# A graph layer and a mixture of experts on one core: one more expert's weights resident, search tables in the weight slots, pools that wait by tile, and a second pair kept for the tail

## The chip, the core and the metric

The kernel runs on one core of a Trainium2 chip. Its engines are TensorE (PE; PEld are its weight loads), VectorE (DVE), ScalarE (ACT), GpSimd (POOL) and SyncE (SP), each with a queue of its own that is worked through in order; SP, ACT and POOL also issue DMAs. The metric is the device time of one execution in microseconds (us), lower is better. The kernel before has a median of 478.54 us in three runs (478.29 to 480.56).

## The reference, cut to what matters

```python
# x (1024, 512); 16384 edges src -> dst with a weight; dst is sorted
HW  = layernorm(x) @ W
agg = segment_sum(edge_weight[:, None] * HW[src], dst) + bias
x   = x + relu(agg)

xt     = layernorm(x)                                # 1024 tokens
scores = sigmoid(xt @ Wg.T + bg)                     # 64 experts
w, idx = top_k(scores, 2);  w = w / w.sum(-1)
nx     = normalize(xt)
h1 = nx @ (gamma_e * W1_e) + (b1_e + beta_e @ W1_e)  # (512, 256) for each expert e
h3 = nx @ (gamma_e * W3_e) + (b3_e + beta_e @ W3_e)
y  = sum over the two chosen e of  w_e * ((silu(h1) * h3) @ W2_e + b2_e)
z  = a small shared expert of width 32 with (gs, bs, Ws1, bs1, Ws3, bs3, Ws2, bs2)
return x + y + z
```

Everything is float32. The experts' weights are 64 x 3 x 0.524 MB, just over 100 MB, each read once.

## The kernel before

**The graph part.** Tokens lie in 8 tiles of 128. The edges are searched in windows with tables (thr_row, diff, below, erows, sm, then d_w, s_w, e_w, blk_i, hi_i, part) that the pool "graph" (gp) holds. DVE writes one-hots of the edges (one_hots, L403 to L408), PE makes dense blocks of the adjacency matrix from them (matrix_group, L495), turns them (L505) and multiplies with H @ W (weighted_sum, L512). Tile by tile follow finish (L527, L528; the layer norm), scores (L556), choose (DVE: the two best experts), rank (how many earlier tokens took the same expert), put (a token's slot with its expert) and slots (one-hots of these). PE sums them (listed, L620) in plist, and from it DVE makes lists (L695) and tokens (L696): for every pair of experts 128 places, 64 for each expert, with the number of the token, or an invalid one where a place stays empty. nx_d in DRAM gets the normalized tokens.

**The expert part** runs over 33 positions n = 0 to 32, in an order written out by hand: 32 pairs of experts, and in position 24 one expert with the first block of tokens that have no place in a pair. Position n is called pair n below, whatever it holds. Each takes these steps:

- load_expert (L707, L708, L710, on SP's queue): W1 and W3 into one slot of tag w13, W2 into one of tag w2. The pool "weights" has AHEAD = 11 slots of each tag. The graph part uses the same slots for its big tables (big is w13, mid is w2), so that the first weights come as these tables are done with; after that a new expert waits until the expert 11 places earlier has been used: its w13 by xph, its w2 by xpy.
- fetch / gather (L721, POOL): 128 rows of nx_d by tokens, into one of four row tiles that are set to zero first (L717), four positions ahead.
- front / scaled: four transposes (L194, PE), then times gamma and plus beta (L733, L735, DVE), two positions ahead.
- hidden: a product for the biases (L746: bias_hm with two terms of the biases in bf16 over 128 partitions, bias_lo with the third over 64; for each of the two experts, so four matmuls), 16 records of xph (L750), silu (L753, ACT), mul (L755, DVE). Matmuls of the two experts of a pair run side by side in the two halves of the array.
- turned: two transposes (L762) and a copy (L764, ACT).
- back(n - 1): outputs of the position before (L772 on PE, 8 records; the copy xy, L775, ACT) and scatter (L779, POOL) of these rows to y_d in DRAM, which has two rows for each token and was set to zero near the start.

In the order of the program, position n has hidden(n), back(n - 1), extra work, turned(n), front(n + 2). Extra work is beyond (n = 2) and beyond_list (n = 4 to 11), which make the lists of tokens without a place, and "other outputs" (other_rows on DVE and ACT, other_turn L904, other_sum L911 and L912): the shared expert and the b2 of one tile, added to res. Two of these eight stand with weights() (the normalized top-2 weights, stored to w_d at L799) before front(0), the other six in three steps each from n = 13.

**The tail.** The last pair is not scattered: block_weights (POOL gathers the weights of its tokens) and block_hots (DVE, eight one-hots of 128 x 128) are made at n = 31. After the loop, y_d is read back in eight pieces (ys, L1010, alternating on ACT's and SP's queue), and waits for the scatter of n = 31. For each tile PE multiplies the one-hots with y (L1014), in odd tiles also a diagonal with ys (L1016); DVE adds the weighted ys rows (L1018, 12 times) and PE's sum (L1020, 8 times), and the tile is stored (L1021). A loop over further blocks without a place does not turn here.

Pools opened after the graph part (bp, gb, lp, psx) lie over the memory of the graph part's pools; their first use waits for those.

Of the kernel before, what the change touches and what calls it, by code (L numbers as in the profile page):

```python
# [9 lines left out]
F32 = mybir.dt.float32  # L10
I32 = mybir.dt.int32
# [7 lines left out]
P = 128  # L19
EPS = 1e-5  # L20
AHEAD = 11
# [3 lines left out]
def kernel(  # L25
# [111 lines left out]

    bias_hm = const.tile([P, 2 * H], BF16, name="bias_hm")
    bias_lo = const.tile([E, 2 * H], BF16, name="bias_lo")
    both = const.tile([P, E], BF16, name="both")  # L140
# [58 lines left out]
    with tc.tile_pool(name="graph", bufs=1) as gp, \  # L199
# [6 lines left out]
        def row_tile(name):  # L206
            return gp2.tile([P, D], F32, name=name, tag="row", bufs=6)

        with tc.manual_schedule(engines={ENG.PE, ENG.DVE, ENG.Activation, ENG.Pool}):

            nc.gpsimd.iota(iota, pattern=[[1, P]], base=0, channel_multiplier=0, allow_small_or_imprecise_dtypes=True)
            thr_row = gp.tile([P, NH, P], F32, name="thr_row")
# [5 lines left out]
            diff = gp.tile([P, P], F32, name="diff")  # L218
# [33 lines left out]
            below = gp.tile([P, NH, P], BF16, name="below")  # L252
# [8 lines left out]
            rows = gp.tile([P, NH, EJ], I32, name="erows")  # L261
# [45 lines left out]
            sm = gp.tile([P, NH, EJ], F32, name="sm")  # L307
# [7 lines left out]
            d_w = gp.tile([P, NH, P], I32, name="d_w")  # L315
            s_w = gp.tile([P, NH, P], I32, name="s_w")
            e_w = gp.tile([P, NH, P], F32, name="e_w")
# [18 lines left out]
            b13 = mid([P, 2, H], "b13", F32)  # L336
            for n in range(2):
                nc.gpsimd.dma_start(b13[n * E:(n + 1) * E, 0, :], b1)
                nc.gpsimd.dma_start(b13[n * E:(n + 1) * E, 1, :], b3)
# [29 lines left out]
            blk_i = gp.tile([P, NH, P], I32, name="blk_i")  # L369
            nc.vector.tensor_scalar(blk_i, d_w, 2, None, op0=ALU.logical_shift_right)  # L370
            nc.vector.tensor_scalar(d_w, d_w, DL - 1, None, op0=ALU.bitwise_and)
            hi_i = gp.tile([P, NH, P], I32, name="hi_i")
            nc.vector.tensor_scalar(hi_i, s_w, 5, None, op0=ALU.logical_shift_right)
            nc.vector.tensor_scalar(s_w, s_w, LO - 1, None, op0=ALU.bitwise_and)
            part = gp.tile([P, 3, NH, P], F32, name="part")
# [50 lines left out]
            row_b = gp.tile([P, P], I32, name="row_b")  # L426
# [56 lines left out]
        with tc.manual_schedule(engines={ENG.PE, ENG.DVE, ENG.Activation, ENG.Pool}):  # L483
# [255 lines left out]
    def hidden(xT, parts):  # L739
# [12 lines left out]
        a1 = bp.tile([P, H], F32, name="xa1")  # L752
        nc.scalar.activation(a1, ph[:, 0, :], AF.Silu)  # L753
        h = bp.tile([P, H], F32, name="xh")
# [3 lines left out]
    def turned(h):  # L758
        pt = psx.tile([P, HC, P], F32, name="xpht")
        v = h.rearrange("t (p c) -> t c p", c=HC)  # L760
        for c in range(HC):
            nc.tensor.transpose(pt[:, c, :], v[:, c, :], ident)  # L762
        hT = bp.tile([P, HC, P], F32, name="xhT")
        nc.scalar.copy(hT, pt)  # L764
        return hT

    def outputs(hT, parts):
# [6 lines left out]
        y = bp.tile([P, D], F32, name="xy")  # L774
# [15 lines left out]
    pick_o = const.tile([P, 1], BF16, name="pick_o")  # L790
# [17 lines left out]
    def beyond():  # L808
# [29 lines left out]
        nc.vector.tensor_mul(one, one, both)  # L838
        picked_o = lp.tile([P, 1], F32, name="picked_o")
        nc.vector.tensor_reduce(picked_o, one, AX.X, ALU.add)  # L840
        nc.vector.tensor_copy(pick_o, picked_o)
# [21 lines left out]
    def beyond_hots(c):  # L863

        hots = []
        for n in range(2):
            so = bp.tile([P, P], F32, name="oso", bufs=4)
# [18 lines left out]
    def other_rows(i):  # L886
        st = bp.tile([P, ZW], F32, name="st")
# [27 lines left out]
    def block_weights(numbers):  # L915
        w = bp.tile([P, 1], F32, name="bw", bufs=1)
# [6 lines left out]
    def block_hots(of, w):  # L923
        row = bp.tile([P, NT], F32, name="brel", bufs=1)
# [150 lines left out]
```

## Time and profile before

| | |
|---|---|
| median of three runs | 478.54 us |
| profiled execution, its own time | 480.64 us |
| its span, first to last instruction | 478.8 us |
| TensorE clock granted, mean | 0.965 |
| PE busy | 437.4 us, 91% of the span |
| DVE busy | 237.9 us, 50% |
| ACT, POOL busy | 97.8 us, 115.5 us |
| DMA | 132.52 MB, mean 277 GB/s |
| pair pace, n = 0 to 32 | 32 periods in 239.5 us |

Times in lines are microseconds from the start of the span. The profile cuts the span into 40 equal slices with a digit for the busy tenths of each engine; further views list what an engine waited for, groups of instructions by line, the chain of work that ended last, and the instructions of a stretch in order of time. In a line of the timeline stand start, duration, engine, line of the code, operation, what is written and read, and in brackets the idle time before it with what ended it. SPq, ACTq and POOLq are the queues' own entries, DMA issues among them.

### The profile page before, as it was taken

The page shows a single profiled execution, that of the slowest core. Times are in us where ns is not written, and L with a number is a line of the kernel's source. Part 1 is how long each engine was busy: PE and PEld are TensorE (multiplying, and loading weights), DVE is VectorE, ACT ScalarE, POOL GpSimd, SP SyncE. Part 2 cuts the span into 40 slices and gives each one's busy share as a digit, 9 for nine tenths or more (in the row PEclk, how much of TensorE's full clock was granted, in tenths as well). Part 3 has the DMA queues.
Part 4 walks back from the last instruction along what each step waited for, and adds up shares of the span by engine and source line. Part 5 has one row for each costly group of instructions (what it writes and reads, how often), then busy time and mean ns, then how long its engine had stood idle before and what let it go on. Part 6 is the DMA issues. An engine that isn't in the chain of part 4 may idle for free. (4 is left out here: it accounts for less than half of the span.)

```text
span 478.8 us, 6941 instructions
## 1 busy us (share of the span) xinstructions
PE 437.4 (91%) x2438; PEld 216.2 (45%) x2438; DVE 237.9 (50%) x725; ACT 97.8 (20%) x224; POOL 115.5 (24%) x148
## 2 busy tenths in 40 slices
PE   2999999999799996588999999999999999999782
PEld 1554995555455554333343443333433334534230
DVE  5979797402787777534743432323332332322265
ACT  1342223223421211101121121121121111211200
POOL 5533100000042223513123323323313323110200
PEclk9999999999999997599899999999999999999977
DMA  8296930232168539338999999999999999999194
GB/s 248 92 123 115 370 138 1 78 100 102 54 233 315 177 113 397 127 115 313 386 396 408 406 406 407 404 409 407 408 404 408 408 405 407 405 410 403 46 365 160
DMA packets 42296, 132.52 MB, mean 277 GB/s; under 512 B 8023, under 2 KB 8151, under 8 KB 42128
## 3 DMA queue, kind: packets, MB, share of 16 engines
q1 hardware_dynamic: 30464, 107.56, 58.4%
q0 software_dynamic: 8304, 18.17, 12.7%
q10 hardware_dynamic: 3488, 6.30, 3.6%
q8 instruction: 20, 0.33, 0.3%
q14 instruction: 20, 0.16, 0.1%
HBM read 124.00 MB, written 18.88 MB: 298 GB/s over the span
## 5 line engine op out<-in xcount | busy, mean ns | idle before, releaser
L750 PE MATMUL xph<-w,xT 128*64 128x512 f32 (+1 forms) x520 | 128.1, 606 | 1.8 <-DMA w<-in_L_ffn_W_dram 1.4
L779 POOL DMA_INDIRECT y_d<-xy,lists x31 | 32.8, 1057 | 168.3 <-ACT xhT L764 68.9
L750 PEld LDWEIGHTS xph<-w,xT 128*64 128x64 f32 (+1 forms) x520 | 39.0, 139 | 69.0 <-issue 66.1
L772 PE MATMUL xpy<-w,xhT 128*64 128x512 f32 (+1 forms) x260 | 67.4, 593 | 0.6 <-ACT xhT L764 0.6
L755 DVE TENSOR_TENSOR xh<-xa,xph 128x256 f32<-128x256 f32 x33 | 13.9, 420 | 106.3 <-ACT xa L753 106.3
L512 PE MATMUL acc<-hw,AT 128*128 128x512 f32 x128 | 60.6, 600 | 0.0
L495 PE MATMUL ph<-ov,ol 128*32 128x128 bf16 x768 | 48.1, 421 | 0.1
L753 ACT ACTIVATE xa<-xph 128x256 f32<-128x256 f32 x33 | 12.6, 383 | 152.9 <-PE xph L750 152.9
L495 PEld LDWEIGHTS <-ol 128*32 128x32 bf16 x768 | 38.0, 144 | 11.6 <-DVE ol L408 2.3
L772 PEld LDWEIGHTS xpy<-w,xhT 128*64 128x64 f32 (+1 forms) x260 | 21.5, 138 | 37.2 <-issue 35.0
L721 POOL DMA_INDIRECT rows<-nx_d,tokens x32 | 34.8, 1086 | 12.4 <-issue 9.1
L297 PE MATMUL ph<-w_sb,hT 128*128 128x512 f32 x64 | 31.2, 637 | 0.7 <-ACT hT L290 0.7
L733 DVE TENSOR_TENSOR xT<-xpt,gT 128x512 f32<-128x512 f32 x32 | 22.0, 686 | 16.2 <-PE xpt L194 15.2
L512 PEld LDWEIGHTS acc<-hw,AT 128*128 128x128 f32 x128 | 22.1, 191 | 17.4 <-issue 17.4
L775 ACT COPY xy<-xpy 128x512 f32<-128x512 f32 x33 | 19.3, 585 | 49.1 <-PE xpy L772 44.1
L735 DVE TENSOR_TENSOR xT<-xT,bT 128x512 f32<-128x512 f32 x32 | 22.2, 693 | 1.1
L612 POOL TENSOR_SCALAR so<-rank_at,here 128x128 f32<-128x128 f32 x14 | 8.9, 635 | 53.2 <-DVE here L603 53.2
L194 PE MATMUL xpt<-ident,rows 128*128 128x128 f32 x132 | 21.5, 288 | 0.0
L522 POOL DMA_DIRECT2D base<-base_d x8 | 4.5, 568 | 68.1 <-DVE res L528 66.7
L499 ACT COPY A<-ph 128x256 f32<-128x256 f32 x32 | 10.4, 377 | 45.7 <-PE ph L495 45.7
L194 PEld LDWEIGHTS xpt<-ident,rows 128*128 128x128 f32 x132 | 19.2, 211 | 1.1 <-issue 0.6
L403 DVE TENSOR_TENSOR ov<-iv,vl 128x2048 bf16<-128x2048 bf16 x16 | 19.5, 1217 | 0.0
(276 smaller groups left out, 489.1 us busy)
## 6 DMA issues: line engine op xcount, KB each, us to landing
w<-in_L_ffn_W_dram SPq DMA_DIRECT2D x195, 512.0 KB
y_d<-zero POOLq DMA_DIRECT2D x1, 4096.0 KB
base_d<-in_L_gnn_bias_dram POOLq DMA_DIRECT2D x1, 2048.0 KB, 18.9
base<-base_d POOLq DMA_DIRECT2D x8, 256.0 KB, 15.2
nx_d<-nx ACTq DMA_DIRECT2D x8, 256.0 KB
ys<-y_d ACTq DMA_DIRECT2D x4, 512.0 KB
ys<-y_d SPq DMA_DIRECT2D x4, 512.0 KB
w_sb<-in_L_gnn_W_dram ACTq DMA_DIRECT2D x1, 1024.0 KB
```

Source lines behind the costliest of these rows:

```text
L194: nc.tensor.transpose(ps[:, k, :], v[:, k, :], ident[:n, :n])
L297: nc.tensor.matmul(ph, hT[:, k, :], w_sb[:, k, :], start=(k == 0), stop=(k == KC - 1))
L403: nc.vector.tensor_tensor(ov, iv, vl[:, 0, h, None, q].to_broadcast([P, P, 16]), ALU.is_equal)
L495: nc.tensor.matmul(pa[LO * wq:LO * (wq + 1), u, :], ol[:, n, :, q], ov[:, :, q], start=(n == 0), stop=(n == 2))
L512: nc.tensor.matmul(accs[t], ATs[h][t // 4][:, t % 4, wq, :], hws[h][:, wq, :], start=(h == 0 and wq == 0), stop=(h == NH - 1 and wq == NQ ...
L721: nc.gpsimd.indirect_dma_start(out=rows, out_offset=None, in_=nx_d[:, :], in_offset=bass.IndirectOffsetOnAxis(ap=of, axis=0), bounds_check ...
L733: nc.vector.tensor_tensor(xT.rearrange(view, n=n), pt.rearrange(view, n=n), g[:, :, :, None].to_broadcast(over), ALU.mult)
L735: nc.vector.tensor_tensor(xT.rearrange(view, n=n), xT.rearrange(view, n=n), b[:, :, :, None].to_broadcast(over), ALU.add)
L750: nc.tensor.matmul(ph[n * r:(n + 1) * r], xT[:, k, n * r:(n + 1) * r], w13[:, :, k, :], start=False, stop=(k == KC - 1))
L772: nc.tensor.matmul(py[n * r:(n + 1) * r], hT[:, c, n * r:(n + 1) * r], w2[:, c, :], start=(c == 0), stop=(c == HC - 1))
L775: nc.scalar.copy(y, py)
L779: nc.gpsimd.indirect_dma_start(out=y_d[:, :], out_offset=bass.IndirectOffsetOnAxis(ap=numbers, axis=0), in_=y, in_offset=None, bounds_chec ...
```

## The change

Six things change together.

1. AHEAD is 12. Memory for it comes from the search tables, which move into weight slots (early in a w2 slot, windows in a w13 slot; row_a and row_b are written over hi_i), and from fewer buffers: row tiles 6 to 5, xa1, xh, xhT and xy 3 to 2, oso 4 to 2, st 3 to 1. bw and brel get 2 instead of 1.
2. The biases are held as three bf16 terms of 32 experts over 96 partitions (bias3, in two halves of the experts), with selectors picks: a pair takes two matmuls instead of four. b13 is loaded by 12 DMAs instead of 4.
3. The pools bp, gb, lp and psx are opened with reuse_waits="tile", gb first: a tile waits for what used its own memory.
4. All eight other outputs stand beside pairs, from n = 6 on; none before front(0). weights() stands in n = 0 after hidden(0).
5. The last two pairs are not scattered. Their block_weights are made at n = 30, their one-hots and two diagonals at n = 32. The ys loads stand on SP behind the last weights and wait for the scatter of n = 30.
6. In the tail PE adds both pairs' blocks of a tile in one PSUM tile, and two diagonal products (for tiles 6 and 7) instead of four; DVE has 14 weighted rows and 8 sums. PSUM tiles go round over four names instead of three.

```diff
-AHEAD = 11
+AHEAD = 12
...
-    bias_hm = const.tile([P, 2 * H], BF16, name="bias_hm")
-    bias_lo = const.tile([E, 2 * H], BF16, name="bias_lo")
-    both = const.tile([P, E], BF16, name="both")
+    EH = E // 2
+    bias3 = const.tile([3 * EH, 2, 2 * H], BF16, name="bias3")
+    picks = const.tile([3 * EH, 2, E], BF16, name="picks")
...
-            return gp2.tile([P, D], F32, name=name, tag="row", bufs=6)
+            return gp2.tile([P, D], F32, name=name, tag="row", bufs=5)
...
-            thr_row = gp.tile([P, NH, P], F32, name="thr_row")
+            early = mid([P, 8, P], "early", F32)
+            thr_row = early[:, :NH]
...
-            diff = gp.tile([P, P], F32, name="diff")
+            diff = early[:, 6]
...
-            d_w = gp.tile([P, NH, P], I32, name="d_w")
-            s_w = gp.tile([P, NH, P], I32, name="s_w")
-            e_w = gp.tile([P, NH, P], F32, name="e_w")
+            windows = big([P, 8, NH, P], "windows")
+            d_w, s_w, blk_i, hi_i = (windows[:, j].bitcast(I32) for j in range(4))
+            e_w = windows[:, 4]
+            part = windows[:, 5:8]
...
-            b13 = mid([P, 2, H], "b13", F32)
-            for n in range(2):
-                nc.gpsimd.dma_start(b13[n * E:(n + 1) * E, 0, :], b1)
-                nc.gpsimd.dma_start(b13[n * E:(n + 1) * E, 1, :], b3)
+            b13 = mid([3 * EH, 2, 2, H], "b13", F32)
+            for n in range(3):
+                for a in range(2):
+                    for m, of in enumerate((b1, b3)):
+                        nc.gpsimd.dma_start(b13[n * EH:(n + 1) * EH, a, m, :], of[a * EH:(a + 1) * EH, :])
...
-            row_a = gp.tile([P, P], I32, name="row_a")
+            row_a, row_b = hi_i[:, 0, :], hi_i[:, 1, :]
...
             def bias_terms():
-                v = b13.rearrange("p a h -> p (a h)")
-                terms = [mid([P, 2 * H], "bterm", BF16) for _ in range(2)]
-                for term in terms:
-                    nc.vector.tensor_copy(term, v)
-                    nc.vector.tensor_sub(v, v, term)
-                nc.vector.tensor_copy(bias_hm[:E, :], terms[0][:E, :])
-                nc.vector.tensor_copy(bias_hm[E:, :], terms[1][E:, :])
-                nc.vector.tensor_copy(bias_lo, v[:E, :])
-                nc.vector.tensor_add(both, ident[:, :E], ident[:, E:])
+                terms = mid([3 * EH, 2, 2 * H], "bterm", BF16)
+                v = b13.rearrange("p a m h -> p a (m h)")
+                for n in range(3):
+                    part = slice(n * EH, (n + 1) * EH)
+                    nc.vector.tensor_copy(terms, v)
+                    nc.vector.tensor_copy(bias3[part], terms[part])
+                    if n < 2:
+                        nc.vector.tensor_sub(v, v, terms)
+                nc.vector.memset(picks, 0.0)
+                for n in range(3):
+                    part = slice(n * EH, (n + 1) * EH)
+                    for a in range(2):
+                        nc.vector.tensor_copy(picks[part, a, a * EH:(a + 1) * EH], ident[part, part])
...
-    bp = ctx.enter_context(tc.tile_pool(name="block", bufs=3))
-    gb = ctx.enter_context(tc.tile_pool(name="rows", bufs=1))
-    lp = ctx.enter_context(tc.tile_pool(name="late", bufs=1))
-    psx = ctx.enter_context(tc.tile_pool(name="ps_x", bufs=2, space=bass.MemoryType.PSUM))
+
+
+    gb = ctx.enter_context(tc.tile_pool(name="rows", bufs=1, reuse_waits="tile"))
+    bp = ctx.enter_context(tc.tile_pool(name="block", bufs=3, reuse_waits="tile"))
+    lp = ctx.enter_context(tc.tile_pool(name="late", bufs=1, reuse_waits="tile"))
+    psx = ctx.enter_context(tc.tile_pool(name="ps_x", bufs=2, space=bass.MemoryType.PSUM, reuse_waits="tile"))
...
-        for terms in (bias_hm, bias_lo):
-            rows = terms.shape[0]
+        for a in range(2):
             for n, (_, pick) in enumerate(parts):
-                nc.tensor.matmul(ph[n * r:(n + 1) * r], pick[:rows].to_broadcast([rows, r]), terms,
-                                 start=(terms is bias_hm), stop=False)
+                if a in pick:
+                    nc.tensor.matmul(ph[n * r:(n + 1) * r], pick[a].to_broadcast([3 * EH, r]), bias3[:, a, :],
+                                     start=(a == min(pick)), stop=False)
         for k in range(KC):
...
-        weights()
-        sts = [other_rows(i) for i in range(2)]
-        sTs = [other_turn(st) for st in sts]
-        for i in range(2):
-            other_sum(i, sTs[i])
         front(0)
         front(1)
 
         hots, st, sT = None, None, None
         for n, q in enumerate(order):
             if q < NP:
-                parts = [(load_expert(nc.sync, W1[e:e + 1], W3[e:e + 1], W2[e:e + 1]), both[:, e:e + 1])
-                         for e in (2 * q, 2 * q + 1)]
+                parts = [(load_expert(nc.sync, W1[e:e + 1], W3[e:e + 1], W2[e:e + 1]),
+                          {e // EH: picks[:, e // EH, e:e + 1]}) for e in (2 * q, 2 * q + 1)]
             else:
                 e = nc.values_load(oexp_i[0:1, 0:1], engines=[ENG.SP], min_val=0, max_val=E - 1)
-                parts = [(load_expert(nc.sync, W1[ds(e, 1)], W3[ds(e, 1)], W2[ds(e, 1)]), pick_o)]
+                parts = [(load_expert(nc.sync, W1[ds(e, 1)], W3[ds(e, 1)], W2[ds(e, 1)]), either)]
             fetch(n + 4)
+            if n == LAST:
+
+                y_of = y_d.rearrange("(i p n) d -> i p n d", p=P, n=2)
+                ys = [wpool.tile([P, 2, 2, D], F32, name="ys", tag="w13")[:, j] for i in range(NT // 2) for j in range(2)]
+                for i in range(NT):
+                    nc.sync.dma_start(ys[i], y_of[i])
+                hots_last = [block_hots(tokens[:, NP - 2 + m:NP - 1 + m], w_last[m]) for m in range(2)]
+                diag = wpool.tile([P, 2, P], F32, name="diag", tag="w2")
+                for j in range(2):
+                    nc.scalar.activation(diag[:, j, :], ident, AF.Copy, scale=wts[:, NT - 2 + j, 1:2])
             h = hidden(xTs.pop(n), parts)
-            back(n - 1)
+            if n < LAST:
+                back(n - 1)
+            else:
+                y_last = [outputs(*hTs.pop(LAST - 1))]
+            if n == 0:
+                weights()
             if n == 2:
...
-            if n >= 13 and (n - 13) // 3 + 2 < NT:
-                i = (n - 13) // 3 + 2
-                if n % 3 == 1:
+            if n >= 6 and (n - 6) // 3 < NT:
+                i = (n - 6) // 3
+                if n % 3 == 0:
                     st = other_rows(i)
-                elif n % 3 == 2:
+                elif n % 3 == 1:
                     sT = other_turn(st)
                 else:
                     other_sum(i, sT)
-            if n == LAST - 1:
-                w_last = block_weights(lists[:, NP - 1:NP])
-                hots_last = block_hots(tokens[:, NP - 1:NP], w_last)
-                diag = wpool.tile([P, NT // 2, P], F32, name="diag", tag="w2")
-                for i in range(1, NT, 2):
-                    nc.scalar.activation(diag[:, i // 2, :], ident, AF.Copy, scale=wts[:, i, 0:1])
+            if n == LAST - 2:
+                w_last = [block_weights(lists[:, NP - 2 + m:NP - 1 + m]) for m in range(2)]
             hTs[n] = (turned(h), parts)
             front(n + 2)
 
-
-        y_of = y_d.rearrange("(i p n) d -> i p n d", p=P, n=2)
-        queues = (nc.scalar, nc.sync)
-        ys = []
-        for i in range(NT):
-            ys.append(wpool.tile([P, 2, D], F32, name="ys", tag="w13"))
-            queues[i % 2].dma_start(ys[i], y_of[i])
-        y = outputs(*hTs.pop(LAST))
-        for i in range(NT):
-            po = psx.tile([P, D], F32, name=("xpt", "xph", "xpy")[i % 3])
-            nc.tensor.matmul(po, hots_last[:, i, :], y, start=True, stop=(i % 2 == 0))
-            if i % 2:
-                nc.tensor.matmul(po, diag[:, i // 2, :], ys[i][:, 0, :], start=False, stop=True)
-            for n in range(i % 2, 2):
+        pos = {}
+
+        def add_block(m, i):
+            if m == 0:
+                pos[i] = psx.tile([P, D], F32, name=("xpt", "xph", "xpy", "xpht")[i % 4])
+            nc.tensor.matmul(pos[i], hots_last[m][:, i, :], y_last[m], start=(m == 0), stop=(m == 1))
+            if m == 0 and i >= NT - 2:
+                nc.tensor.matmul(pos[i], diag[:, i - NT + 2, :], ys[i][:, 1, :], start=False, stop=False)
+
+        def add_rows(i):
+            for n in range(2 if i < NT - 2 else 1):
                 nc.vector.scalar_tensor_tensor(res[:, i, :], ys[i][:, n, :], wts[:, i, n:n + 1], res[:, i, :],
                                                op0=ALU.mult, op1=ALU.add)
-            nc.vector.tensor_add(res[:, i, :], res[:, i, :], po)
+
+        def add_sums(i):
+            nc.vector.tensor_add(res[:, i, :], res[:, i, :], pos.pop(i))
             queues[i % 2].dma_start(out[i * P:(i + 1) * P, :], res[:, i, :])
+
+        queues = (nc.scalar, nc.sync)
+        add_block(0, 0)
+        y_last.append(outputs(*hTs.pop(LAST)))
+        add_block(0, 1)
+        for i in range(2):
+            add_rows(i)
+        for i in range(NT):
+            add_block(1, i)
+            if i + 2 < NT:
+                add_block(0, i + 2)
+                add_rows(i + 2)
+            add_sums(i)
```

More of the change, by code (lines that the diff above doesn't have):

```diff
@@ L251 @@
             nc.vector.tensor_copy(first, dst_i[:, 0:1])
-            below = gp.tile([P, NH, P], BF16, name="below")
+            below = early[:, 7].bitcast(BF16).rearrange("p (h q) -> p h q", h=NH)
             nc.vector.tensor_scalar(below, thr_row, first, None, op0=ALU.is_gt)
@@ L260 @@
             nc.vector.tensor_copy(row_i, row)
-            rows = gp.tile([P, NH, EJ], I32, name="erows")
+            rows = early[:, 2:4].bitcast(I32)
             for h in range(NH):
@@ L304 @@
             scales(0, 3)
-            sm = gp.tile([P, NH, EJ], F32, name="sm")
+            sm = early[:, 4:6]
             for h in range(NH):
@@ L365 @@
             times_w(3)
-            blk_i = gp.tile([P, NH, P], I32, name="blk_i")
             nc.vector.tensor_scalar(blk_i, d_w, 2, None, op0=ALU.logical_shift_right)
             nc.vector.tensor_scalar(d_w, d_w, DL - 1, None, op0=ALU.bitwise_and)
-            hi_i = gp.tile([P, NH, P], I32, name="hi_i")
             nc.vector.tensor_scalar(hi_i, s_w, 5, None, op0=ALU.logical_shift_right)
             nc.vector.tensor_scalar(s_w, s_w, LO - 1, None, op0=ALU.bitwise_and)
-            part = gp.tile([P, 3, NH, P], F32, name="part")
             nc.vector.scalar_tensor_tensor(part[:, 0], d_w, float(HI), hi_i, op0=ALU.mult, op1=ALU.add)
@@ L421 @@
             ohs = [one_hots(0, 0)]
-            row_a = gp.tile([P, P], I32, name="row_a")
+            row_a, row_b = hi_i[:, 0, :], hi_i[:, 1, :]
             nc.vector.tensor_scalar(row_a, at_i, 3, None, op0=ALU.logical_shift_right)
             nc.vector.tensor_scalar(row_a, row_a, 7, None, op0=ALU.bitwise_and)
-            row_b = gp.tile([P, P], I32, name="row_b")
             nc.vector.tensor_sub(row_b, at_i, row_a)
@@ L751, in hidden @@
                                  start=False, stop=(k == KC - 1))
-        a1 = bp.tile([P, H], F32, name="xa1")
+        a1 = bp.tile([P, H], F32, name="xa1", bufs=2)
         nc.scalar.activation(a1, ph[:, 0, :], AF.Silu)
-        h = bp.tile([P, H], F32, name="xh")
+        h = bp.tile([P, H], F32, name="xh", bufs=2)
         nc.vector.tensor_mul(h, a1, ph[:, 1, :])
@@ L762, in turned @@
             nc.tensor.transpose(pt[:, c, :], v[:, c, :], ident)
-        hT = bp.tile([P, HC, P], F32, name="xhT")
+        hT = bp.tile([P, HC, P], F32, name="xhT", bufs=2)
         nc.scalar.copy(hT, pt)
@@ L773, in outputs @@
                                  start=(c == 0), stop=(c == HC - 1))
-        y = bp.tile([P, D], F32, name="xy")
+        y = bp.tile([P, D], F32, name="xy", bufs=2)
         nc.scalar.copy(y, py)
@@ L789 @@
     b_o = const.tile([P, KC, 1], F32, name="b_o")
-    pick_o = const.tile([P, 1], BF16, name="pick_o")
+    pick_o = const.tile([3 * EH, 2, 1], BF16, name="pick_o")
+    either = {a: pick_o[:, a, :] for a in range(2)}
     novf_i = const.tile([1, 1], I32, name="novf_i")
@@ L837, in beyond @@
             nc.vector.tensor_reduce(to[:, :, 0], each, AX.X, ALU.add)
[L838 to L841, printed above, removed]
+        pick = lp.tile([3 * EH, 2, E], F32, name="pick")
+        nc.vector.tensor_tensor(pick, picks, one[:3 * EH, None, :].to_broadcast([3 * EH, 2, E]), ALU.mult)
+        picked_o = lp.tile([3 * EH, 2], F32, name="picked_o")
+        nc.vector.tensor_reduce(picked_o, pick, AX.X, ALU.add)
+        nc.vector.tensor_copy(pick_o[:, :, 0], picked_o)
         eoh = lp.tile([P, NT * 2, E], BF16, name="eoh")
@@ L866, in beyond_hots @@
         for n in range(2):
-            so = bp.tile([P, P], F32, name="oso", bufs=4)
+            so = bp.tile([P, P], F32, name="oso", bufs=2)
             nc.vector.tensor_scalar(so, rank_at, oslot[:, c, n:n + 1], None, op0=ALU.is_equal)
@@ L886, in other_rows @@
     def other_rows(i):
-        st = bp.tile([P, ZW], F32, name="st")
+        st = bp.tile([P, ZW], F32, name="st", bufs=1)
         tmp = bp.tile([P, E], F32, name="stt", bufs=1)
@@ L915, in block_weights @@
     def block_weights(numbers):
-        w = bp.tile([P, 1], F32, name="bw", bufs=1)
+        w = bp.tile([P, 1], F32, name="bw", bufs=2)
         nc.gpsimd.memset(w, 0.0)
@@ L923, in block_hots @@
     def block_hots(of, w):
-        row = bp.tile([P, NT], F32, name="brel", bufs=1)
+        row = bp.tile([P, NT], F32, name="brel", bufs=2)
         nc.vector.tensor_copy(row[:, 0:1], of)
@@ L1033 @@
         nc.vector.tensor_copy(b_o, bT[:, :, ds(e, 1)])
-        nc.vector.tensor_copy(pick_o, both[:, ds(e, 1)])
-        parts = [(experts, pick_o)]
+        nc.vector.tensor_copy(pick_o, picks[:, :, ds(e, 1)])
+        parts = [(experts, either)]
         gather(rows_of[0], of)
```

## The prediction, made before the changed kernel ran

> **What bounds the kernel now.** I read the 40 slices first, then the waits of SP (the queue that issues all weights), then stretches of the timeline. Of the slices, rows PE, granted clock, DMA and GB/s:
>
> ```profile
> PE   2999999999799996588999999999999999999782
> PEclk9999999999999997599899999999999999999977
> DMA  8296930232168539338999999999999999999194
> GB/s 248 92 123 115 370 138 1 78 100 102 54 233 315 177 113 397 127 115 313 386 396 408 406 406 407 404 409 407 408 404 408 408 405 407 405 410 403 46 365 160
> ```
>
> A slice is 12 us. Up to slice 15 (190 us) PE is full and DMA is not. From slice 19 on both are, at 404 to 410 GB/s: weights arrive as fast as anywhere in this profile. Two holes cost time: slices 16 to 18 (192 to 228 us), the passage from the graph part to the experts, and the last three, the tail. Of the windows (PE, PEld, DVE, ACT, POOL busy, granted clock, DMA share, GB/s) three steady or broken stretches:
>
> ```profile
> 198.00:202.00 4.00, 3.91 (x6) 1.74 (x7) 0.73 (x3) 0.27 (x1) 3.09 (x4) 0.50 0.30 92
> ...
> 312.00:336.00 24.00, 24.00 (x120) 9.37 (x117) 7.50 (x17) 4.86 (x13) 6.54 (x6) 1.00 1.03 407
> ...
> 450.00:456.00 6.00, 2.56 (x11) 0.80 (x10) 0.00 (x0) 0.86 (x2) 1.00 (x1) 0.94 0.25 54
> 456.00:462.00 6.00, 5.30 (x7) 2.18 (x8) 2.85 (x4) 0.58 (x1) 0.00 (x0) 0.50 1.02 417
> ```
>
> So the stream of weights sets the pace of 312 to 336. That it, and not PE, is late shows in SP's timeline:
>
> ```profile
> 186.96 0.33 SPq L710 DMA_DIRECT2D w<-in_L_ffn_W_dram  x1
> 208.06 0.33 SPq L707 DMA_DIRECT2D w<-in_L_ffn_W_dram  x1
> ...
> 215.98 0.33 SPq L710 DMA_DIRECT2D w<-in_L_ffn_W_dram  x1
> ```
>
> Eleven experts are loaded by 187; the twelfth's W1 and W3 wait for pair 0's xph, its W2 for pair 0's xpy. Among SP's waits (total, times, longest) this is the first of
>
> ```profile
> SPq L707 <- PE xph L750: 19.8, 1, 19.8
> ...
> SPq L1010 <- DMA y_d<-xy,lists: 17.8, 1, 17.8
> ```
>
> (the second belongs to the tail). From 215.98 it runs without a gap to the last weights, which land at 444.7 (call this T0). The tail, in the timeline:
>
> ```profile
> 444.82 3.22 PE L750 MATMUL xph<-w,xT 128*64 128x512 f32 x13 [0.34 <-DMA w<-in_L_ffn_W_dram]
> ...
> 451.13 1.00 POOL L779 DMA_INDIRECT y_d<-xy,lists  x1 [5.39 <-ACT xhT L764]
> ...
> 458.89 1.54 DVE L1018 SCALAR_TENSOR_TENSOR res<-ys,wts,res 128x512 f32<-128x512 f32 x2 [9.29 <-DMA ys<-y_d]
> ...
> 473.31 0.69 DVE L1020 TENSOR_TENSOR res<-res,xph 128x512 f32<-128x512 f32 x1
> ```
>
> and in the chain that ended last (start, duration, what), the two last scatters from issue to landing:
>
> ```profile
> 443.32 2.41 DMA y_d<-xy,lists
> ...
> 451.13 2.67 DMA y_d<-xy,lists
> ```
>
> The scatter of pair 31 (451.13 to 453.8) holds back the reading of y_d; PE falls idle and comes back at clock 0.50; DVE then works from 458.9 to 474.0 almost without pause, and the span ends 4.8 us later.
>
> **What the Trainium skill says.** "TensorE: Matmul & The Clock Gate", Part 1: after idleness TensorE runs at half rate until it has been busy for a window of some 3.4 us. The trace agrees: 0.50 in 198 to 202 and in 456 to 462, a block matmul (L1014) 0.86 us at full clock and 1.7 at half. "DMA: Bandwidth & Descriptors", section "Anatomy of one DMA — SWDGE (gpsimd) path": a fixed cost of about 2 us; the scatter above takes 2.67 from issue to landing. Same page, "Rules for kernel authors": more issuing queues add no bandwidth; here 417 GB/s with two queues (456 to 462) against 407 with SP alone. So ys on SP alone is free.
>
> **The change, part by part** (times on the clock of before).
>
> *Twelfth expert.* 3 x 0.524 = 1.573 MB leave the stream after the restart and go before 190, where DMA has idle slices. At 407 GB/s: **-3.9 us**. SP's order doesn't change; the twelfth's three loads come behind the eleven's and wait for the last graph tables in their slots. The search tables are the new risk: early is last used near 34 us, windows near 40 (row_a and row_b a little later), by DVE and PE work well ahead of 175, when the last six loads start. At worst they cost the whole gain.
>
> *One bias product.* Two bf16 matmuls per position go (the two of a form run side by side, so one step of 0.33 us): 33 x 0.33 = 10.9 us of PE. PE was full too, so this keeps PE below the stream: a bare pair takes 6.88 us (209.91 to 216.80), afterwards 6.55; with the other outputs and the beyond lists about 231 us of PE against 235.7 us of stream left. The gain itself is therefore booked at **0**; the slack is 4.5 us. Eight DMAs more on POOL's queue (b13, 8 x 0.53 = 4.3 us near 43 to 47) delay zb and the zeroing of y_d; POOL's next urgent work, the base loads, is at 116. bias_terms takes some 7.9 us of DVE against 3.4, under an idle stretch of 21 us (94.4 to 116). Both 0; without cover 4 us each.
>
> *Pools waiting by tile, other outputs beside pairs.* Now the four memsets (L717, 2.03 us) start when all of the graph part's pools are free, 192.80; DVE mixes weights, other_rows and tile 7's choose and put; tokens stand at 196.31, the first gather at
>
> ```profile
> 192.80 2.03 POOL L717 MEMSET rows<- 128x512 f32 x4 [2.69 <-DMA w<-in_L_ffn_W_dram]
> ...
> 197.29 1.12 POOL L721 DMA_INDIRECT rows<-nx_d,tokens  x1 [2.46 <-DVE stt L891]
> ```
>
> Afterwards the memsets wait only for the scores' matmuls (189.3), and DVE runs choose and put alone: tile 6 took 2.98 us for them, tile 7 4.58 with the rest mixed in; the memset also slowed DVE (L599 0.50 against 0.17; "GPSIMD Engine Reference", section "Key points": the two share SBUF interfaces). I take 1.2 for the tokens and 0.2 for the interfaces: gather near 195.9. The two other outputs before pair 0 (L904, L911, 4.7 us of PE) hid the gather's landing and warmed the clock; without them the transposes and bias of pair 0 run at 0.50. Gain 1.4, cold clock +0.4, two biases saved before xpy(0) -0.6: restart at 214.3, **-1.6 us**. Bounds: -3 (full clock) and +1.5 (cold through all of xph(0), 3.65 more, less the gains). The Silu table load (1.28 us at 194.38) moves ahead of pair 0's silu, where ACT is idle. weights()' seven DVE ops and its DMA to w_d (0.38 on ACT's queue) now stand between silu(0) and xhT(0): xhT(0) has 4.5 us until its matmuls at 214.06. Two more others beside pairs: 2 x 1.3 us of PE, out of the slack; their DVE ops (1.2 + 0.69 each) lie in DVE that is busy 7.5 of 24 us.
>
> *Two tail pairs.* T0 moves by -3.9 - 1.6 = -5.5. Relative to T0: the ys loads stood at T0+9.1 behind scatter 31; afterwards they wait for scatter 30, which landed at 445.73 (T0+1.0), are 4.19 MB at 417 GB/s, and are in by T0+11.5, the first by T0+3. Behind them on SP are only the stores of odd tiles. Their four slots hold experts used long before. New before xph(32): 16 bhots by DVE (16 x 0.27 = 4.3 us from about 441.3, done 445.6; the mul that follows needs DVE at 448.4), two diag copies on ACT, a second block_weights on POOL at pair 30 (one memset, one gather of 1.1 us, idle there). PE goes from xpy(31) through block 0 to xpy(32) without the pause of 3.6 us, so at full clock; xy(32) stands at T0+9.7. Then 15 blocks and 2 diag products, 17 x 0.86 = 14.6 us of PE, end at T0+23.6 with the waits, the last add on DVE at T0+24.6. DVE alone: 14 x 0.765 + 8 x 0.69 = 16.2 us from T0+6.7 would end at T0+22.9. Before it was T0+29.3. **-4.7 us**. Bounds: -6.4 (DVE bound) and +1 (PE at 0.50 for a window, 3.4 us lost, and later ys).
>
> **Sum:** -3.9 - 1.6 - 4.7 = -10.2 us. The profiled execution took 480.64 us, its span 478.8, so 1.84 lie outside the span; it is 2.1 above the median of 478.54. Span 468.6, plus 1.84 is 470.5 for such an execution; taken off the median, about **468.5**.
>
> **Rivals.** *The stage is bound by PE or its clock, not the stream.* Before, one idle gap of 1.9 us (223.0 to 224.9) was followed by a half-clock xph of 5.33 instead of 3.65; two of these eat the slack. Then the early expert brings nothing: -1.6 - 4.7 and half of 3.9 lost, 472 to 474. For it: PE is 24.00 of 24. Against it: the bias products leave. *The tail pays little,* since PE there does 18 products where it did 12: at half clock for one window 471 to 473. *More:* the restart is -3 and the tail DVE bound: 464 to 465. *Slower:* a table's slot is released late, and SP's in-order queue stops behind it, so that loads meant for the idle time before 187 go after the restart. Each expert so shifted costs 3.9 us; the gains are worth 10.2, so it decides from 2.6 experts; four make 484. For it: SP's waits on slots are up to 39.4 us long already. Against it: tables die before 50 us, and the last slots wait for late work (L495, L620) as before. That the change doesn't do what it says would show as eleven experts loaded before the restart: 472.5.
>
> **How the numbers follow.** Forecast 0.55; the PE-bound stage 0.14; a poor tail 0.13; more gain 0.09; late slots 0.09, of which half end above 480.9. 0.5%, 2.4 us, is about what a measurement can tell from no change. Faster 0.91, same 0.04, slower 0.05. The range takes the bounds of restart and tail: 463.5 to 474.5.
>
> **What would show it.** Right: twelve experts issued before 190; SP's next weights near 206 and 214; 407 GB/s to T0 near 439; L1010 issued about 1 us after T0; PE at full clock from T0 to the end, DVE ending T0+24.6. Wrong: a wait of SP for a search table or b13 beyond 100 us; PE idle with clock below 0.9 between 216 and 440; gaps in the tail's DVE row put down to xpt or xph; GB/s under 400 in the steady slices.

## The result and the profile after

The changed kernel has a median of 472.99 us in four runs; the kernel before has 479.55 in its four, one more than were known ahead. The ratio is 0.985 with a 95% interval of 0.980 to 0.990. Run once more in a later series (e5_again) it stood at 0.983 (0.979 to 0.987). By the medians it is faster by 6.6 and 7.1 us, and the intervals allow about 5 to 10. The time lies inside the range, 4.5 us above the forecast of 468.5, which had expected a gain of 10. Times and ratios here and below are those of runs in the fast state; one of the six runs of e3_onetail, at 810.25 us, was slow and is left out.

The profiled execution took 473.35 us, its span 471.5 against 478.8. The same slices as before (rows PE, granted clock, DMA, GB/s, here of 11.8 us):

```profile
PE   2999999999699996288699999999999899899994
PEclk9999999999999998579889999999999999999998
DMA  8265770430178829546989999999999999999683
GB/s 256 90 119 122 264 263 1 164 106 0 44 247 310 296 76 365 219 138 214 412 341 400 407 408 406 408 408 408 406 407 406 408 408 405 408 408 411 256 315 113
```

The reader is to see two things. The tail has the clock at 9 up to the last slice (8), where its last two slices had 7. And the passage to the experts (slices 16 to 20, counted from 0) is no better than it was: PE has a 2 where it had a 5, the clock 5 and 7, and in slice 20 the stream falls from 412 to 341 GB/s after it had been full.

SP's timeline tells where the stream starts again and ends:

```profile
186.43 0.33 SPq L714 DMA_DIRECT2D w<-in_L_ffn_W_dram  x1
208.36 0.33 SPq L711 DMA_DIRECT2D w<-in_L_ffn_W_dram  x1
...
215.81 0.33 SPq L714 DMA_DIRECT2D w<-in_L_ffn_W_dram  x1
...
432.34 0.33 SPq L714 DMA_DIRECT2D w<-in_L_ffn_W_dram  x1
```

Twelve experts are in before the gap, but the restart is at 208.36 and 215.81, where it was at 208.06 and 215.98. Cut at five events the two spans compare so (us; each stretch from its timeline; "steady" is the third weight issue after the gap, the first W2, which waits for xpy(0)):

| stretch | before | after | difference |
|---|---|---|---|
| start to MAX8 of the last token tile | 189.54 | 189.75 | +0.2 |
| to tokens | 6.77 | 6.65 | -0.1 |
| to steady | 19.67 | 19.41 | -0.3 |
| to the issue of the last weights | 219.71 | 216.53 | **-3.2** |
| to the end of DVE's last sum | 38.31 | 33.74 | **-4.6** |
| to the end of the span | 4.80 | 5.42 | +0.6 |

The restart, for which the forecast had 1.6 us, gave 0.2. First the lines of the kernel before, from MAX8 of the last token tile to the last weights:

```profile
189.54 0.23 DVE L565 MAX8 top<-score 128x8 f32<-128x64 f32 x1 [1.69 <-ACT score L559]
190.13 0.17 DVE L567 CAST expert<-idx 128x2 f32<-128x2 uint32 x1
...
193.39 0.50 DVE L599 CAST pair<-pair_i 128x2 f32<-128x2 uint32 x1
...
201.83 1.49 PE L194 MATMUL xpt<-ident,rows 128*128 128x128 f32 x8
...
204.38 3.65 PE L750 MATMUL xph<-w,xT 128*64 128x512 f32 x16 [0.38 <-issue]
...
435.69 0.33 SPq L710 DMA_DIRECT2D w<-in_L_ffn_W_dram  x1
```

The timeline of the changed kernel shows what became of the gain:

```profile
190.25 1.92 POOL L721 MEMSET rows<- 128x512 f32 x4
190.34 1.85 DVE L565 CAST expert<-idx 128x2 f32<-128x2 uint32 x1
...
196.40 0.18 DVE L698 TENSOR_SCALAR tokens<-lists 128x32 int32<-128x32 int32 x1
...
200.75 1.98 PE L193 MATMUL xpt<-ident,rows 128*128 128x128 f32 x8 [4.61 <-DMA rows<-nx_d,tokens]
...
203.38 4.98 PE L754 MATMUL xph<-w,xT 128*64 128x512 f32 x16
```

The memset does start 2.5 us earlier. There it meets DVE in the middle of choose: a cast of 128x2 elements, 0.17 us in the kernel before, ends only when the memset ends. The kernel before did not show so long a stop: a cast of the same form (L599) took 0.50 us beside its memset and ended 0.9 us before it; why the two differ is open. And PE, without the other outputs, has been idle for 4.6 us when the rows of pair 0 arrive, and most of xph(0) runs at half clock (4.98 us instead of 3.65). In the chain of work that ended last both the cast and a later xph at half clock are links (start, duration, what):

```profile
190.34 1.86 DVE expert L565
...
236.38 5.38 PE xph L754 x16
```

That xph, of pair 4, is the third loss. The windows (PE, PEld, DVE, ACT, POOL, clock, DMA share, GB/s):

```profile
228.00:234.00 6.00, 2.84 (x14) 0.70 (x10) 5.76 (x15) 0.97 (x2) 1.87 (x2) 0.95 1.03 407
234.00:240.00 6.00, 5.74 (x18) 2.55 (x20) 2.39 (x7) 0.37 (x1) 0.17 (x1) 0.50 1.03 408
240.00:246.00 6.00, 6.00 (x34) 2.64 (x32) 2.31 (x8) 1.34 (x3) 1.23 (x2) 0.99 0.76 289
...
300.00:420.00 120.00, 116.12 (x542) 47.52 (x540) 40.05 (x94) 22.93 (x62) 34.25 (x33) 1.00 1.03 407
```

DVE works off beyond (some 10 us behind pair 2), PE waits 3.4 us for mul(3), comes back cold, frees slots late, and 6 us later the stream has a hole (DMA share 0.76 instead of 1.03). From 246 on the share is 1.03 again, and PE has idle time. In the kernel before PE waited 1.05 us at this place, and the share stayed at 1.00 or more from 222 on, at 370 and 385 GB/s in 234 to 246:

```profile
234.70 0.50 PE L762 MATMUL xpht<-ident,xh 128*128 128x128 f32 x2 [1.05 <-DVE xh L755]
```

The tail in the timeline:

```profile
441.49 3.22 PE L754 MATMUL xph<-w,xT 128*64 128x512 f32 x13 [0.83 <-DMA w<-in_L_ffn_W_dram]
443.18 4.16 SPq L982 DMA_DIRECT2D ys<-y_d  x8
447.57 1.13 PE L1021 MATMUL xpt<-xy,bhots 128*128 128x512 f32 x2 [0.28 <-ACT xy L779]
...
464.33 1.02 PE L1021 MATMUL xpht<-xy,bhots 128*128 128x512 f32 x2
465.39 0.69 DVE L1031 TENSOR_TENSOR res<-res,xpht 128x512 f32<-128x512 f32 x1 [0.17 <-PE xpht L1021]
```

From the last weights (441.5) to the end of DVE's last sum (466.1) it is 24.6 us, where it was 29.2: after one wait of 0.28 us PE goes through without a pause at 0.86 us a block, and DVE's last sum waits for it.

### The profile page after: what moved, and what is told of

It reads as the page before. It is cut to its first block, busy times and chain, and to the rows that moved or that the text cites. A ratio compares the mean times of both kernels' runs of the same rounds, so it can differ in the third digit from the quotient of the medians.

```text
span 471.5 us, 6849 instructions
## 1 busy us (share of the span) xinstructions
PE 427.2 (91%) x2386; PEld 212.3 (45%) x2386; DVE 248.2 (53%) x744; ACT 97.2 (21%) x222; POOL 118.7 (25%) x157
## 4 chain that ended last, share of the span: by engine, by line
PE 63%; DMA 17%; DVE 8%; issue 1%; ACT 0%; DVEq 0%; POOLq 0%; ACTq 0%; SPq 0%
PE xph L754 17%; DMA w<-in_L_ffn_W_dram 16%; PE acc L510 11%; PE ph L493 10%; PE xpy L776 8%; PE xpt L193 2%; PE pt L503 2%; PE ph L554 2%; PE xph L750 1%; PE xpht L766 1%; PE xpy L917 1%; PE xpy L884 1%; PE xpt L1021 1%; PE xph L1021 1%; PE xpht L1021 1%
## 5 line engine op out<-in xcount | busy, mean ns | idle before, releaser
L754 PE MATMUL xph<-w,xT 128*64 128x512 f32 (+1 forms) x520 | 129.4, 607 | 5.3 <-DMA w<-in_L_ffn_W_dram 5.2
L754 PEld LDWEIGHTS xph<-w,xT 128*64 128x64 f32 (+1 forms) x520 | 41.8, 140 | 71.0 <-issue 64.3
L783 POOL DMA_INDIRECT y_d<-xy,lists x30 | 31.6, 1054 | 157.4 <-DMA y_d<-xy,lists 81.5
L493 PEld LDWEIGHTS <-ol 128*32 128x32 bf16 x768 | 36.6, 144 | 13.2 <-issue 3.7
L766 PEld LDWEIGHTS xpht<-ident,xh 128*128 128x128 f32 x66 | 11.7, 212 | 18.3 <-DVE xh L759 8.5
```

The costliest lines, as they stand in the source:

```text
L493: nc.tensor.matmul(pa[LO * wq:LO * (wq + 1), u, :], ol[:, n, :, q], ov[:, :, q], start=(n == 0), stop=(n == 2))
L754: nc.tensor.matmul(ph[n * r:(n + 1) * r], xT[:, k, n * r:(n + 1) * r], w13[:, :, k, :], start=False, stop=(k == KC - 1))
L783: nc.gpsimd.indirect_dma_start(out=y_d[:, :], out_offset=bass.IndirectOffsetOnAxis(ap=numbers, axis=0), in_=y, in_offset=None, bounds_chec ...
```

## The experiments

There were three series, each on one chip together with the kernel before: e1 to e4, e5 to e8, and e9 to e12. Across series the ratios are the safer comparison. Differences of a microsecond in the medians lie within the intervals; there the stretches of the profiles help. The graph part varies by up to 2.7 us between the profiled executions (MAX8 at 188.9 to 191.6), so stretches are counted from an event, not from the start.

Stretches scatter too. e3 differs from the changed kernel in the tail alone, so up to there its profile is a third one of the changed kernel. From steady to the last weights the three take 216.53, 217.40 (e5) and 215.77 us (e3), from MAX8 to the last weights 242.6, 243.5 and 241.5. A difference inside such a spread shows nothing.

### One part undone

**e1_ahead11:** `AHEAD = 12` back to `AHEAD = 11`.

> The changed kernel with AHEAD 11 instead of 12, all else kept. Theory (the stream of weights at 407 GB/s sets the pace from the restart to the last weights): 1.573 MB more stand behind the restart, so the last weights land 3.5 to 3.9 us later and the time is 476 to 477 us against 473.0. Rival (PE and its half-clock stretches set the pace, the stream has slack): the last weights land within 1 us of where they do now, 473 to 474 us.

477.67 us, 0.991 (0.989 to 0.993), a little more than the theory had. Steady to last weights: 219.82 us, against 215.77 to 217.40 in the three profiles of the changed kernel, and 219.71 before. So the twelfth expert is worth 2.4 to 4.1 us in this stretch, and about 3 to 4 by the ratios (0.991 against 0.985 and 0.983). The rest of the change shows no net effect in this stretch.

**e2_bias4:**

```diff
-        for a in range(2):
+        for terms in (bias_hm, bias_lo):
...
-                if a in pick:
-                    nc.tensor.matmul(... pick[a].to_broadcast([3 * EH, r]), bias3[:, a, :], ...)
+                nc.tensor.matmul(... pick[:rows].to_broadcast([rows, r]), terms, ...)
```

> The changed kernel with the four bias matmuls of before in each position (bias_hm, bias_lo, both), all else kept: 0.33 us more of PE for each of 33 positions, 10.9 us. Theory (stream bound, the bias product only gives PE slack): PE of the changed kernel shows 3.9 us idle in 300 to 420 us, some 6 from 246 to the last weights; 8.9 us more in these 27 positions overfill that by about 3, and 6 positions before the stream is full add up to 2: 475 to 478 us. Rival A (PE has slack enough): 473. Rival B (PE bound all through): 10.9 us more, 484 us.

473.13 us, 0.983 (0.980 to 0.985): rival A. Two windows of it:

```profile
234.00:240.00 6.00, 5.00 (x26) 2.22 (x28) 3.31 (x8) 0.96 (x2) 2.04 (x2) 1.00 1.00 353
...
300.00:420.00 120.00, 119.85 (x573) 47.09 (x572) 39.58 (x94) 23.31 (x63) 33.16 (x33) 1.00 1.03 406
```

PE is full in 300 to 420, and the stream runs at 406 GB/s all the same: the 10.9 us of PE just fit. My figure of a 3 us overfill was wrong, and so was the 2 us for the positions before: steady comes only 0.65 us later. And since PE is busier while DVE works off beyond, it waits 1.07 us for mul(3), as in the kernel before, instead of 3.41: it was the smaller bias product that lengthened this wait. The half-clock stretch comes earlier (clock 0.86 in 222 to 234), and 234 to 240 is at full clock. Two small effects may cancel here; e12 takes them apart.

**e3_onetail:** the tail of before (one pair not scattered, ys behind the last scatter, four diagonals).

> The changed kernel with the tail of before: only the last pair not scattered, ys read behind the scatter of pair 31, four diagonals. Theory: from the last weights to the end of the span 34.1 us as before, against 30.1 in the changed kernel: 477 us, PE idle and at half clock again behind the last xpy. Rival (the tail is bound by DVE's 20 to 22 passes and the stores either way, the earlier ys bring nothing): 473 to 474.

476.18 us, 0.989 (0.986 to 0.992). From the last weights (440.5) to the end of DVE it is 28.9 us against 24.6. PE falls idle and cold as before:

```profile
446.00:452.00 6.00, 2.21 (x10) 0.56 (x9) 0.00 (x0) 1.35 (x3) 1.00 (x1) 0.94 0.36 104
452.00:458.00 6.00, 5.94 (x7) 2.52 (x8) 3.27 (x5) 0.01 (x1) 0.00 (x0) 0.50 1.02 416
```

To the end of the span it is 33.9 us against 30.0, the 4 us that were expected.

**e6_poolwaits:** `reuse_waits="tile"` taken from the four pools. **e7_front_others:** weights() and two other outputs back ahead of front(0), with st in two buffers for it. **e5_again:** the changed kernel beside them.

> The changed kernel as it is, to stand beside the others of this series: its first measurement was 0.985 of the kernel before, 474 us where that takes 481. In the profile tokens at 196.4, a hole in the stream near 240, and 30.1 us from the last weights to the end of the span.

> The changed kernel with the four pools opened without reuse_waits (they wait for all of the graph part's pools), all else kept. Theory (POOL's memset stands in the way of DVE): the memset starts later, near 192.5, so DVE's cast of expert takes about 0.2 us instead of 1.85 and small operations during the memset some tenths more; tokens at 195 to 195.6, time 0.5 to 1.5 us less than the changed kernel. Rival (waiting by tile is what it was put in for): memset and gather later, tokens as now or later, 1 to 2 us more.

> The changed kernel with weights() and two of the other outputs ahead of front(0) as in the kernel before, six beside pairs from n = 12. Theory (the restart gains nothing because the clock is cold for pair 0 as well as by the cast): PE is warm for pair 0 (xph(0) 3.65 us instead of 4.98), but the other outputs lie in front of the transposes and DVE's part of them between put and tokens; first weights behind the restart between 207.5 and 209, time within 1 us of the changed kernel. Rival (the two others cost their 4.7 us of PE on the path): restart 3 us later, time 3 us more.

e5 473.35 us, 0.983 (0.979 to 0.987). e6 474.46 us, 0.987 (0.983 to 0.991), neither of what was expected: memset and cast stand as in the changed kernel (the cast 1.85), so it is not the waiting by tile that brings the memset forward; gb stands first in both, and which other part of the change does it was not tried. Steady comes 3 us later from tokens, 22.42 instead of 19.44, for a reason that I had not seen:

```profile
207.63 1.28 ACT L757 ACT_TABLE_LOAD   x1 [18.62 <-PE xph L754]
```

Silu's table load waits with pair 0's xph and lies on the path. In the changed kernel it ran in ACT's idle time:

```profile
189.84 1.28 ACT L757 ACT_TABLE_LOAD   x1
```

PE then waits 2.37 us for mul(0) instead of 0.94, and is cold for pair 1, from the timeline of e6:

```profile
209.81 0.51 PE L766 MATMUL xpht<-ident,xh 128*128 128x128 f32 x2 [2.37 <-DVE xh L759]
...
210.97 5.30 PE L754 MATMUL xph<-w,xT 128*64 128x512 f32 x16
```

1.4 us of waiting and 1.7 of xph (3.60 in the changed kernel) make the 3. Waiting by tile is worth about that at steady. At the last weights, counted from MAX8, e6 is 2.0 to 4.0 us behind (245.5 us against 241.5 to 243.5); the medians differ by 1.1 us, within the intervals.

e7 473.79 us, 0.985 (0.980 to 0.989), within 1 us as the theory had it, but at another price: the first weights leave 12.80 us after tokens instead of 11.99, yet there is no hole (DMA share 1.02 or more from 228 on; PE waits 1.70 us for mul(3)), steady to last weights falls to 214.54, and the last weights leave at 433.36 where e5 has 433.53, though its graph part was 1.6 us slower. In these two profiles a later restart and a hole are worth the same; the medians cannot tell.

### The three losses taken away

**e4_zero_act:**

```diff
-    for rows in rows_of:
-        nc.gpsimd.memset(rows, 0.0)
+    for n, rows in enumerate(rows_of):
+        nc.scalar.activation(rows, res[:, n, :], AF.Copy, scale=0.0)
```

> The changed kernel with the four row tiles set to zero by ACT (a copy of res times 0) instead of POOL's memset. Theory (the memset at 190.25 to 192.17 holds DVE's cast of expert, 1.85 us instead of 0.2, and so the tokens): the cast takes about 0.2 us, tokens stand at 194.7 instead of 196.4, the first weights behind the restart leave 1.6 us earlier, near 206.7, and the time is 471.2 to 471.6 us. Rival (DVE's cast waits for something else, or the gain is lost behind DVE's block of beyond at 222 to 233): tokens at 196.4, or the hole in the stream near 240 grows by the same, 473 us.

470.51 us, 0.978 (0.975 to 0.981).

```profile
189.26 2.20 ACT L721 ACTIVATE rows<-res 128x512 f32<-128x512 f32 x4
...
189.90 0.17 DVE L565 CAST expert<-idx 128x2 f32<-128x2 uint32 x1
...
194.28 0.18 DVE L698 TENSOR_SCALAR tokens<-lists 128x32 int32<-128x32 int32 x1
```

The cast takes 0.17, MAX8 to tokens 4.97 instead of 6.65: the collision is the cause. From MAX8 to the issue of the last weights it is 239.7 us instead of 241.5 to 243.5 in the three profiles of the changed kernel, so at least these 1.7 arrive; the hole at 240 to 246 is smaller here as well (0.91).

**e8_beyond3:** beyond cut in three.

```diff
             if n == 2:
                 beyond()
+            if n == 3:
+                beyond_expert()
+            if n == 4:
+                beyond_blocks()
```

> The changed kernel with DVE's block of beyond (11 us at 222 to 233 behind pair 2) cut in three, behind pairs 2, 3 and 4, and the lists two positions later. Theory (the block makes PE wait 1.9 and 3.4 us, then run pair 4 at half clock, and so opens the hole of about 1.4 us in the stream at 240 to 246): no PE idle over 1 us and clock 1.00 in 216 to 246, DMA share above 0.95 from 222 on, last weights 1.4 us earlier counted from the restart, time 1 to 1.5 us less. Rival (the twelve resident experts carry the stream over the block anyway): the hole moves or closes without effect, no difference.

471.93 us, 0.982 (0.978 to 0.986); its stretches:

```profile
228.00:234.00 6.00, 6.00 (x32) 2.25 (x31) 5.00 (x14) 1.10 (x3) 2.04 (x2) 1.00 1.03 407
234.00:240.00 6.00, 6.00 (x32) 2.50 (x32) 5.76 (x16) 1.25 (x3) 1.60 (x2) 1.00 1.03 407
240.00:246.00 6.00, 6.00 (x32) 2.37 (x30) 2.36 (x7) 1.24 (x3) 1.55 (x2) 1.00 1.03 408
```

PE, clock and stream are full, so the block of DVE made the hole. What closing it is worth is not shown: steady to last weights is 215.71, at the edge of the changed kernel's own spread (215.77 to 217.40), and the medians (471.93, 473.35) differ by 1.4 us, within the intervals.

**e9_warm** (e4 and three matmuls, of two records each, in PE's idle time ahead of front(0)), **e10_best** (e9 and e8):

```diff
+        pz = psx.tile([P, D], F32, name="xpy")
+        for _ in range(3):
+            nc.tensor.matmul(pz, ident, res[:, 0, :], start=True, stop=True)
         front(0)
```

> As e4_zero_act (rows set to zero by ACT), with three matmuls of ident and res into an unread PSUM tile ahead of front(0), where PE waits for the first gather; they change nothing of the output. Theory (after the cast, the cold clock is the second thing that eats the restart): transposes, bias and xph of pair 0 at full clock, 2 us less from tokens to the first weights behind the restart (10.5 us instead of 12.5), time 1.5 to 2 us below e4. Rival (the stream has a hole behind beyond near 240 which takes up an earlier restart): the restart comes earlier, the last weights don't; time as e4.

> As e9, with beyond cut in three as in e8_beyond3. Theory (cast 1.7, clock 2, hole 1.4 add up, because the stream is then without a hole from the restart on): last weights 5 us earlier than in the changed kernel, 468 to 469 us where that takes 473.4. Rival (each of them is partly the same slack): not below 470.

e9 469.76 us, 0.978 (0.974 to 0.981). Pair 0 runs at full clock:

```profile
193.63 4.85 PE L967 MATMUL xpy<-res,ident 128*128 128x512 f32 x6
198.60 1.52 PE L193 MATMUL xpt<-ident,rows 128*128 128x128 f32 x8
200.05 0.41 PE L750 MATMUL xph<-bias,picks 96*64 96x512 bf16 x2
200.82 3.72 PE L754 MATMUL xph<-w,xT 128*64 128x512 f32 x16 [0.37 <-DVE xT L739]
```

Tokens to the first weights fall from 12.47 us in e4 (11.96 in the changed kernel) to 10.42, and MAX8 to the last weights from 239.7 to 237.9. How much of this reaches the time is not shown: the medians differ by 0.8 us, where 1.5 to 2 were expected, the ratios are the same, and the profiled execution of e9 (468.25) was its fastest by 1.4 us.

e10 468.32 us, 0.975 (0.971 to 0.978): 5.0 us less than e5 in time, 4.0 by the ratios, and within the 468 to 469 of the theory. MAX8 to the last weights is 237.6, where that execution of e9 has 237.9, so the two profiles cannot say what the cut of beyond adds. The medians give it 1.4 us, as they did between e5 and e8, both times within the intervals; whether it is its own stays open.

**e11_best_onediag:** in add_block `i >= NT - 2` becomes `i >= NT - 1`, and add_rows gives DVE both rows of tile 6.

> As e10, with one diagonal product less in the tail (tile 6; its second weighted row goes to DVE, 15 instead of 14). Theory (the tail is bound by PE: 18 products of 0.86 us without a pause, DVE idle some 3 us in it): DVE's end 0.6 to 0.9 us earlier from the last weights, 0.5 to 0.9 us less. Rival (DVE ends the tail): the same or 0.7 later.

467.43 us, 0.973 (0.969 to 0.976), 0.9 below e10. Last weights to the end of DVE 23.7 us instead of 24.6, by one diagonal of 0.86: the tail is bound by PE. This is the fastest kernel measured, 2.7% below the kernel before.

**e12_best_bias4:** e10 with the four bias matmuls.

> As e10, with the four bias matmuls of before. In e2 they cost nothing, but there they also covered DVE's block of beyond and closed the hole. Theory (stream bound; the bias product gives slack that nobody uses): pairs before the stream is full 0.33 us longer each, restart 0.7 later, last weights at most 1 us later; time within 1 us of e10. Rival (without the hole to hide in, the 10.9 us of PE show): 3 us or more over e10.

469.21 us, 0.977 (0.974 to 0.980), 0.9 above e10:

```profile
300.00:420.00 120.00, 119.57 (x566) 48.78 (x562) 38.79 (x89) 23.11 (x61) 32.67 (x31) 1.00 1.03 407
```

The stretch from steady to the last weights is 214.78 against 214.74 in e10; only steady itself is 0.4 later, counted from tokens. The 10.9 us of PE are not on the path, with or without the hole.

## Why the prediction was right, and where it was off

Sign and range held, and the two largest terms of the sum with them. The span fell by 7.3 us where the sum had 10.2; most of the difference is the restart, and then the time behind DVE's last sum.

- *Twelfth expert, -3.9.* Measured 2.4 to 4.1 in the profiles and 3 to 4 by the ratios (e1), so the size held. The load left the stream as said, and the stream does set the pace (407 GB/s with PE idle for 3.9 of 120 us). The hole near 240 takes nothing from this term, since e1 has it too (DMA share 0.77).
- *One bias product, 0.* Right; e2 and e12 bound it to about 1 us. The slack that it gives is not even needed: with four products PE has 0.15 us (e2) and 0.43 us (e12) idle in 120, and the stream runs at 406 and 407 GB/s. The rival of a PE-bound stage fell with this.
- *Pools by tile and others moved, -1.6.* This step failed: 0.2 measured. Its largest part, the gather 1.4 us earlier, came to nothing (issued at 197.38 instead of 197.29). The prediction cited the shared interfaces of DVE and POOL, priced them at 0.2 us by the slowed operations around 193, and credited this as a gain because the memset would leave that place. It did not ask what DVE does where the memset goes. The cast there cost 1.7 (e4). "GPSIMD Engine Reference", section "8. Key points", speaks of contention; in this place it was a stop for the rest of the memset. Nor was it the waiting by tile that moved the memset (e6). The cold clock was priced at 0.4, for the transposes and the biases; xph(0) was cold too, 1.3 us more, which the prediction had only as a bound. That tokens to the first weights took just 0.2 us more than before is luck: with the other outputs gone the transposes began 3.4 us after the gather's issue instead of 4.5, a gain that was not booked. Against a warm clock the restart lost 1.5 us in the changed kernel and 2.0 in e4 (e9). The Silu table load was placed right, in ACT's idle time; that it stays there hangs on the waits by tile (e6).
- *The gap behind beyond.* The prediction saw the idle gap and the half-clock xph behind beyond, and used them only for a rival. With a smaller bias product the wait before mul(3) grew from 1.05 us to 3.4 (1.07 with four products, e2). "TensorE: Matmul & The Clock Gate", Part 1, says that an idle window of about 3.4 us brings the half rate; the clock of 0.50 in 234 to 240 and the xph of 5.6 us instead of 3.6 agree with it. The gap of 1.9 us is shorter than that window, and was followed by the half rate in the kernel before and not in the changed one (xph(3) there took 3.60 us). So the rival's mechanism was real, but it opened a hole in the stream rather than making PE the bound.
- *Two tail pairs, -4.7.* Measured -4.6 to the end of DVE, with T0+24.6 as forecast; e3 alone gives 4.3 there, and e11 shows the bound by PE. The 0.6 us that came after DVE's last sum (5.42 instead of 4.80) were not foreseen; 5.4 to 5.7 in all kernels with the new tail, 5.0 in e3, and its cause stays open. The sum for PE does not come out as written: T0+9.7 and 14.6 us are T0+24.3, not T0+23.6; PE ended at T0+23.9, because one of the 17 products ran before xy(32) was ready.
- *Slower by late slots.* SP had no wait for a search table; all twelve experts were issued by 186.43. This rival is out.
- *Signs and range.* Of the signs of being wrong one came, the idle PE with a clock under 0.9 between 216 and 440. Of those of being right three missed: the weights behind the gap left at 208.36 and 215.81 instead of near 206 and 214, T0 was 441.5 instead of 439, and the ys loads were issued 1.7 us after T0 instead of 1. The bounds of restart and tail, added to the twelfth expert, give 465 to 477, not the 463.5 to 474.5 of the range.

## What to carry to other kernels

When a piece of work is started earlier, price it by what runs at the place where it arrives, on every engine that it can hold up (here DVE's cast behind POOL's memset), and not only by what it leaves. Work that looks idle-filling on PE can be what brings its clock back (xph(0) 3.65 us with it, 4.98 without); if it is moved, put something in its place or count pair 0 at half rate. Where a stream of loads sets the pace, what counts is when it restarts and whether it has holes; less work for PE behind it brought under 1 us here (e12), and lengthened a wait elsewhere.

## What the runs showed of the hardware that was not expected

- A cast of 128x2 elements on DVE took 1.85 us beside a memset of four 128x512 tiles by POOL (1.92 us), ending within 0.02 us of it, and 0.17 us when ACT wrote the same tiles in 2.20 us. In the kernel before a cast of the same form took 0.50 us beside such a memset.
- Loading ACT's table (1.28 us) moved by 18 us with the waits ahead of pair 0's silu: hidden at 189.84, on the path at 207.63 with pools that wait as a whole, where steady came 3 us later, 1.4 by waiting and 1.7 by the cold clock that followed.
